# A two-layer graph-attention kernel: the normed input turned by transfers, elu tile by tile from PSUM as h + 1, guards of two heads together, and a plan with other durations

## The chip, the cores and the metric

The kernel runs on one core of one Trainium2 chip. Its time is the device time of one execution in microseconds (us). Five engines work side by side, each in the order of its own queue: TensorE (PE, matmuls), VectorE (DVE), ScalarE (ACT), GpSimd (POOL) and SyncE (SP, which only issues transfers here). A matmul accumulates in one of eight PSUM banks; everything else on the core lies in SBUF.

## The reference, cut to what matters

The input x is (32, 512, 512) in float32, adj is (32, 512, 512) in int32. There are 32 graphs ("batches"), each of 512 nodes with 512 features. Two layers follow each other, and each adds its result to x:

```python
# layer 0
h = relu(layernorm(x))
s = leaky_relu(h @ w_src [:, None] + h @ w_dst [None, :] + b)      # 512 x 512 scores
x = x + softmax(where(adj + eye, s, -inf), axis=-1) @ h
# layer 1: two graph-attention layers, the first with 4 heads of 256 features
h = relu(layernorm(x))
h = elu(gat(h, adj > 0 or eye, W1, heads=4, concat) + b1)          # 512 x 1024
x = x + gat(h, adj > 0 or eye, W2, heads=1) + b2                   # 512 x 512
```

A `gat` projects (h @ W), takes two scores per node and head from the projection, builds leaky_relu(a_src + a_dst) for every pair of nodes, masks it, applies softmax over the sources, and multiplies the weights with the projection. elu(v) is v for v > 0 and exp(v) - 1 below.

## The kernel before, in words

**Tiling.** The 512 nodes of a batch are T = 4 tiles of 128 rows. All matmuls are float32, and each shows in the trace as two instructions.

**Stages of a batch**, by the names of the functions and of the plan's parts:

- `layer0_scores` (S0): layernorm of x (`layernorm`, L555), the normed tiles (`relu_normed`, L573), two dot products per tile, the masks (`masks0`), then `guards` and `edge_weights`.
- `layer0_out` (O0): `attend` multiplies the edge weights with h and adds to x.
- `layer1_in` (I1): layernorm again, the normed tiles `hn`, and their transpose `hT`: four PSUM banks, each filled by four TensorE transposes (`pe_transpose`, L553) and copied out by `evict` (L582: ACT at L586 or DVE at L592, whichever the plan chooses). POOL adds b2 to x (L914), and SP spills x to DRAM.
- `masks1` (M1): loads adj by a transfer on POOL's queue (L802), compares it (L855), clears the diagonal blocks tile by tile (L861), and turns it by a transposing transfer (L812).
- `layer1_project` (P1) and `layer2_project` (P2): the products with W1 and W2 in `products` (L935). It computes a product of 2 x 2 quarters with seven quarter products in place of eight; the sums S1, S2, S3 and S4 of quarters of the left side are made at L968 (DVE) or L969 (POOL), the sums of the weights once at the start (`sums`). Results leave PSUM by `evict` or an addition (L1001).
- `layer1_scores` (S1) and `layer1_head` (H), for each of four heads. In `layer1_head` a tile of 512 x 257 is aggregated at L760 (257th column: the sum of the weights); L1062 takes its reciprocal and L1065 scales, adds b1 and writes `v`. Two tiles share one `v`. elu then works on 512 columns at a time: for heads 0 to 2 (`TURNED`) exp, relu(1 - e) and a maximum (L1079, L1082, L1086), and the result is turned by a transfer; for head 3 exp(v - 1) of v + 1 and a minimum-maximum (L1101, L1105), which gives h + 1, then TensorE transposes, and the eviction takes the 1 off.
- `layer2_out` (O2): `attend` with the second projection, and the store.

**A turn by transfer** (`turned`, L598): ACT packs the 32-bit values into two 16-bit halves (L605), SP issues a transposing transfer (L612), ACT puts the halves together (L621).

**Guards.** `guards` (L682) finds, per node, a bound of the scores, so that the exponent can't overflow: L687 scales the scores, L698 takes a maximum over the masked scores for each tile, L705 and L710 make the guard from it for each head. `in_lines` transposes the guard on TensorE (L652) and stores it as a line, `row_of` loads it back on every partition (L669), and `edge_weights` subtracts it from the mask on POOL (L736), adds the scores on DVE (L741) and takes the exp on ACT (L748).

**The order.** No engine's order is written by hand. Every operation is recorded with its engine (or a choice of two), a duration and the buffers it touches; `Plan.draft` (L160) plays it through once with these durations and always takes, on the engine that is free first, the ready operation of the lowest rank. A rank is the TensorE work recorded before it, less a lead from the table `LEADS` (L52) for its part. The durations are small formulas (`on_pe`, `on_dve`, `on_act`, `by_dma`, ...) or written at the operation: the adjacency load has 8000 ns, or 16000 ns for early ones (L802). Operations marked `lock` on DVE and POOL exclude each other in the draft. Every buffer kind has a fixed number of places (`slots`): 11 of `big` (8 KB per partition: h, hT, projections, edge weights, sums), 4 of `v`, 8 PSUM banks `acc`. Batches overlap: while batch b runs its heads, batch b + 1 runs O0 and I1, batch b + 2 runs S0, and batch b - 1 runs P2 and O2.

## Time and profile before

| what | value |
|---|---|
| time of the runs | 3639.89, 3628.97 and 3638.29 us; median 3638.29 |
| the profiled execution: its own time | 3638.24 us |
| its span, first to last instruction | 3636.5 us |
| granted TensorE clock, mean | 0.994 |
| instructions | 49863 |
| data moved | 412.60 MB, mean 113 GB/s |

The profile lists busy time per engine ("PE" matmuls, "PEld" weight loads that overlap them). A group's line names the source line, engine and operation, the buffers written and read, the count, the busy time in us, the mean in ns, the idle time of the engine ahead of the group, and what ended most of it. A wait's line gives engine, line and what it waited for, then the total in us, the number of times and the longest. A chain's line gives the start and the duration in us of one piece of the work that ended last. A line of the windows gives the stretch, its length, the busy time of PE, PEld, DVE, ACT and POOL (with instruction counts), the granted clock, the share of the DMA engines and GB/s. Means of short instructions include a part that overlaps with the one before.

### The profile page before, as it was taken

The page shows a single profiled execution, that of the slowest core. Times are in us where ns is not written, and L with a number is a line of the kernel's source. Part 1 is how long each engine was busy: PE and PEld are TensorE (multiplying, and loading weights), DVE is VectorE, ACT ScalarE, POOL GpSimd, SP SyncE. Part 2 cuts the span into 40 slices and gives each one's busy share as a digit, 9 for nine tenths or more (in the row PEclk, how much of TensorE's full clock was granted, in tenths as well). Part 3 has the DMA queues.
Part 4 walks back from the last instruction along what each step waited for, and adds up shares of the span by engine and source line. Part 5 has one row for each costly group of instructions (what it writes and reads, how often), then busy time and mean ns, then how long its engine had stood idle before and what let it go on. Part 6 is the DMA issues. An engine that isn't in the chain of part 4 may idle for free.

```text
span 3636.5 us, 49863 instructions
## 1 busy us (share of the span) xinstructions
PE 3487.2 (96%) x16404; PEld 2998.4 (82%) x16404; DVE 2834.7 (78%) x7596; ACT 1891.2 (52%) x3204; POOL 1500.9 (41%) x1394
## 2 busy tenths in 40 slices
PE   3999999999999999999999999999999999999999
PEld 2788888888888888888888888888888888888888
DVE  7997777877777777777777887877787778787775
ACT  2474455555455544555445655545554555554463
POOL 4444334444334443344433444433445334444341
PEclk9999999999999999999999999999999999999999
DMA  6435344443444443444434444344444344444332
GB/s 178 102 95 131 82 125 113 122 124 110 95 114 128 114 112 92 114 128 116 123 87 122 121 122 121 107 98 114 132 121 123 90 120 114 125 119 124 87 111 64
DMA packets 529827, 412.60 MB, mean 113 GB/s; under 512 B 350904, under 2 KB 390048, under 8 KB 529568
## 3 DMA queue, kind: packets, MB, share of 16 engines
q1 hardware_dynamic: 495776, 375.86, 37.3%
q0 software_dynamic: 33792, 33.56, 6.0%
q8 instruction: 129, 2.11, 0.2%
q14 instruction: 130, 1.06, 0.1%
HBM read 290.72 MB, written 68.28 MB: 99 GB/s over the span
## 4 chain that ended last, share of the span: by engine, by line
PE 76%; DVE 10%; DMA 9%; issue 2%; POOL 1%; ACT 0%; SPq 0%; POOLq 0%; DVEq 0%
PE acc L988 37%; PE acc L760 36%; DMA m<-in_adj_dram 8%; DVE junk L698 3%; PE acc L553 2%; DVE big L741 2%; PE acc L652 1%; DMA big<-lines 1%; DVE x L778 1%; DVE col L705 1%; DVE guard L710 1%; DVE st L559 1%; POOL big L736 1%; DVE v L1086 1%; DVE m L855 1%
## 5 line engine op out<-in xcount | busy, mean ns | idle before, releaser
L760 PE MATMUL acc<-big,big 128*128 128x257 f32 (+1 forms) x8192 | 1876.2, 381 | 61.7 <-DVE v L1065 47.8
L760 PEld LDWEIGHTS acc<-big,big 128*128 128x128 f32 x8192 | 1540.8, 190 | 307.1 <-DVE v L1065 59.9
L736 POOL TENSOR_TENSOR big<-m,big 128x512 f32<-128x512 bf16 x768 | 889.6, 1186 | 667.6 <-DMA big<-lines 455.9
L988 PE MATMUL acc<-w_T,big 128*128 128x258 f32 (+1 forms) x3072 | 776.4, 382 | 1.6 <-DVE big L968 1.6
L988 PE MATMUL acc<-w,big 128*128 128x258 f32 (+1 forms) x3072 | 769.2, 381 | 0.9 <-POOL big L969 0.6
L586 ACT COPY big<-acc 128x258 f32<-128x258 f32 (+2 forms) x650 | 248.7, 383 | 871.9 <-PE acc L988 868.8
L748 ACT ACTIVATE big<-big,ac 128x512 f32<-128x512 f32 x768 | 539.9, 719 | 265.6 <-DVE big L741 258.0
L988 PEld LDWEIGHTS acc<-w_T,big 128*128 128x128 f32 x3072 | 582.4, 191 | 91.3 <-DVE big L968 2.0
L988 PEld LDWEIGHTS acc<-w,big 128*128 128x128 f32 x3072 | 572.1, 190 | 87.1 <-ACT big L586 1.0
L741 DVE SCALAR_TENSOR_TENSOR big<-acc,ac,big 128x512 f32<-128x512 f32 x768 | 555.6, 738 | 23.7 <-POOL big L736 20.7
L698 DVE CUSTOM_DVE_ANT_0 junk<-m,acc 128x512 bf16<-128x512 bf16 x768 | 525.1, 684 | 18.5 <-DVE ac L687 0.4
L969 POOL TENSOR_TENSOR big<-big,big 128x512 f32<-128x512 f32 x128 | 187.3, 1464 | 677.1 <-DVE big L968 667.8
L1001 DVE TENSOR_TENSOR big<-acc,big 128x258 f32<-128x258 f32 (+1 forms) x576 | 243.8, 423 | 257.8 <-PE acc L988 219.6
L605 ACT COPY row<-v 128x1024 uint16<-128x1024 uint16 x192 | 199.4, 1041 | 117.1 <-DVE v L1086 113.7
L988 PE MATMUL acc<-w_-T,big 128*128 128x258 f32 (+1 forms) x1024 | 254.3, 380 | 1.9 <-DVE big L1001 1.9
L778 DVE SCALAR_TENSOR_TENSOR x<-acc,r,x 128x256 f32<-128x256 f32 x512 | 237.4, 477 | 21.1 <-PE acc L760 17.7
L1065 DVE SCALAR_TENSOR_TENSOR v<-acc,r,b_r 128x256 f32<-128x256 f32 x512 | 246.0, 481 | 7.4
L586 ACT COPY flat<-acc 8x128 f32<-8x128 f32 (+2 forms) x188 | 48.0, 255 | 357.7 <-PE acc L652 357.7
L621 ACT COPY big<-v 128x1024 uint16<-128x1024 uint16 x192 | 222.3, 1158 | 3.1 <-DMA v<-row 3.0
L988 PEld LDWEIGHTS acc<-w_-T,big 128*128 128x128 f32 x1024 | 191.5, 189 | 33.7 <-DVE big L1001 3.4
L576 ACT ACTIVATE big<-x,col,col 128x512 f32<-128x512 f32 x256 | 195.7, 804 | 23.2 <-DVE col L568 20.4
L1062 DVE RECIPROCAL r<-acc 128x1 f32<-128x1 f32 x512 | 83.9, 164 | 154.7 <-PE acc L760 152.8
(75 smaller groups left out, 2655.2 us busy)
## 6 DMA issues: line engine op xcount, KB each, us to landing
big<-lines SPq DMA_DIRECT2D x380, 256.0 KB
row<-lines SPq DMA_DIRECT2D x190, 256.0 KB
x<-in_x_dram SPq DMA_DIRECT2D x32, 1024.0 KB
m<-in_adj_dram POOLq DMA_DIRECT2D x64, 512.0 KB, 6.9
spill<-x SPq DMA_DIRECT2D x32, 1024.0 KB
x<-spill SPq DMA_DIRECT2D x32, 1024.0 KB
out_dram<-x SPq DMA_DIRECT2D x30, 1024.0 KB
v<-row SPq DMA_TRANSPOSE x192
```

Source lines behind the costliest of these rows:

```text
L586: nc.scalar.copy(dst_of(), src_of())
L605: lambda: nc.scalar.copy(e.at.bitcast(U16).rearrange("p (b f) -> p b f", b=2), values_of().bitcast(U16).rearrange("p (f b) -> p b f", b=2)),
L621: nc.scalar.copy(out.bitcast(U16).rearrange("p k t (n b) -> p k t n b", b=2), values_of().bitcast(U16).rearrange("p (b t k n) -> p k t n b ...
L698: lambda t=t, amax=amax, a_row=a_row: nc.vector.tensor_tensor_reduce(by_blocks(junk), mask_row(mask_max, t), by_blocks(a_row.at), 1.0, LOW ...
L736: lambda t=t: nc.gpsimd.tensor_sub(by_blocks(E.at[:, t, :]), mask_row(mask, t), by_blocks(g_at())),
L741: lambda t=t: nc.vector.scalar_tensor_tensor(E.at[:, t, :], c_row.at, ac.at[:, 4 + j, t : t + 1], E.at[:, t, :], op0=ALU.max, op1=ALU.add),
L748: lambda t=t: nc.scalar.activation(E.at[:, t, :], E.at[:, t, :], AF.Exp, bias=ac.at[:, 2 * j, t : t + 1]),
L760: lambda s=s: nc.tensor.matmul(acc.at[:, :n], E.at[:, s, node_block(t)], of(s), start=(s == 0), stop=(s == T - 1)),
L778: lambda acc=acc, r=r, f=f, t=t: nc.vector.scalar_tensor_tensor(X.at[:, t, f], acc.at[:, :HD], r.at, X.at[:, t, f], op0=ALU.mult, op1=ALU. ...
L988: lambda k=k: nc.tensor.matmul(acc.at[:, :width], at[a]()[:, k, node_block(r)], weight_of(w, k, c), start=(first and k == 0), stop=(k == n ...
L1001: op("DVE", on_dve(width), lambda: nc.vector.tensor_add(place(), acc.at[:, :width], place()), acc(0) + token, token)
L1065: lambda i=i, v=v, acc=acc, r=r: nc.vector.scalar_tensor_tensor(v.at[:, i, :], acc.at[:, :F], r.at, b1_r[:, h * F : (h + 1) * F], op0=ALU. ...
```

## The change

- **Input turned by transfers.** In `layer1_in` each normed tile goes through `turned`; the TensorE transposes and their evictions go.
- **elu a tile at a time, h + 1.** In `layer1_head` every tile of 256 columns is scaled within its PSUM bank (b1 + 1 is added, for all heads), ACT writes exp(. - 1) to `v`, and DVE makes min(v, 1) max the bank: h + 1. The eviction of head 3 no longer subtracts. What the 1 adds to the layer-2 projection is a constant per column, taken off elsewhere: `column_sums` makes the column sums of W2 once by matmul, subtracts them from b2, and its share of the scores, `kappa`, enters layer 2's guards as a shift.
- **Guards of all heads of a call together**: L705's and L710's operations work on both heads at once. The diagonal blocks of a mask are one operation.
- **Places.** The sums of quarters get 6 places of their own (`sum`), `big` has 9, `v` 6, `guard` 8. In `products` two row blocks go through the seven products side by side, on two banks each.
- **The plan.** Leads are given per part (each head its own) and engine; the lock applies to more small operations, and an operation that finds the lock taken is put back; several durations differ (adjacency load 10400 ns and 12600 ns for the first, reciprocal, matmul, score sums). `EARLY` goes. The recording of layer 2's score columns moves ahead of the first `layer1_in`. The branches for `BY_HALVES` and `STATS_BY_ACT` are not used (an empty tuple, and False).

The diff, cut to its core:

```diff
-            rank.append(work - 1e3 * self.LEADS[lead])
+            rank.append(work - 1e3 * self.LEADS.get(lead, 0.0))
...
+            if locks and e in lock and lock["POOL" if e == "DVE" else "DVE"] > at:
+                heapq.heappush(later[e], (lock["POOL" if e == "DVE" else "DVE"], rank[i], i))
+                continue
...
-    one = 2 * max(0.8376 * n + 2, 110.0)
+    one = 2 * max(0.84 * n + 3, 110.0)
...
-        "big": places("big", 11, [P, T * 2 * XL]),
-        "v": places("v", 4, [P, 2, F]),
+        "big": places("big", 9, [P, T * 2 * XL]),
+        "v": places("v", 6, [P, 2, F]),
+        "sum": places("sum", 6, [P, 2, HN]),
...
+    def column_sums():
+        half = KH // 2
+        lo, hi = Buffer("acc"), Buffer("acc")
...
+                    lambda acc=acc, q=q, k=k, at=at, last=len(of) - 1: nc.tensor.matmul(
+                        acc.at[:, :W2], one.to_broadcast([P, P]), w2_s[q][:, k, :],
+                        start=(at == 0), stop=(at == last),
...
+        op(
+            "DVE", on_dve(n * T + 60), lambda: nc.vector.tensor_add(z.at[:, :n, :], ac.at[:, 1 : 2 * n : 2, :], amax.at[:, :n, :]),
+            scores + amax(*every), z(0), lock=True,
+        )
...
-            "POOL", (1100.0, 11000.0) if first else (2200.0, 16000.0 if early else 8000.0), lambda: nc.gpsimd.dma_start(m.at, node_tiles(adj, b)),
+            "POOL", (1100.0, 12600.0) if first else (2200.0, 16000.0 if early else 10400.0), lambda: nc.gpsimd.dma_start(m.at, node_tiles(adj, b)),
...
-        for t in range(T):
-            own = node_block(t)
-            op(
-                "DVE", on_dve(P), lambda t=t, own=own: nc.vector.tensor_mul(m1.at[:, t, own], m1.at[:, t, own], off_diag),
-                m1(t), m1(t), lock=True,
-            )
+        op(
+            "DVE", on_dve(T * P + 70),
+            lambda: nc.vector.tensor_mul(own_blocks(m1), own_blocks(m1), off_diag.rearrange("p (o n) -> p o n", o=1).to_broadcast([P, T, P])),
+            m1(*ROW), m1(*ROW), lock=True,
+        )
...
+        if TURN_INPUT:
             for t in range(T):
-                pe_transpose(
-                    pt, lambda t=t, pt=pt: pt.at[:, node_block(t)], hn(t) + hT("place"),
-                    lambda t=t, k=k: hn.at[:, t, node_block(k)], ident, t,
-                )
-            evict(pt(*ROW), hT(*((k, t) for t in ROW)), lambda pt=pt: pt.at, lambda k=k: hT.at[:, k, :], N)
+                turned(
+                    lambda t=t: hn.at[:, t, :D], both(hn, t), hT("place"),
+                    lambda t=t: hT.at[:, :, node_block(t)].rearrange("p k (t n) -> p k t n", n=P), hT(*((k, t) for k in range(KD))),
+                )
...
-                lambda i=i, v=v, acc=acc, r=r: nc.vector.scalar_tensor_tensor(
-                    v.at[:, i, :], acc.at[:, :F], r.at, b1_r[:, h * F : (h + 1) * F], op0=ALU.mult, op1=ALU.add
+                lambda acc=acc, r=r: nc.vector.scalar_tensor_tensor(
+                    acc.at[:, :F], acc.at[:, :F], r.at, b1_r[:, h * F : (h + 1) * F], op0=ALU.mult, op1=ALU.add
                 ),
-                acc(0) + r(0) + W["b1"](h), v(i),
+                acc(0) + r(0) + W["b1"](h), acc(0),
+            )
+            op(
+                "ACT", on_act(F, 1),
+                lambda i=i, v=v, acc=acc: nc.scalar.activation(v.at[:, i, :], acc.at[:, :F], AF.Exp, bias=minus_one), acc(0), v(i),
+            )
+            op(
+                "DVE", on_dve(F),
+                lambda i=i, v=v, acc=acc: nc.vector.scalar_tensor_tensor(
+                    v.at[:, i, :], v.at[:, i, :], 1.0, acc.at[:, :F], op0=ALU.min, op1=ALU.max
+                ),
+                acc(0) + v(i), v(i),
             )
...
+            pairs = [[Buffer("acc"), Buffer("acc")] for r in range(T // 2)]
+            for which, a, w, begin, then, i, j in (
+                (0, "A11", "11", True, taken, 0, 0),
+                (1, "S1", "T1", True, taken, 1, 1),
+                (0, "S2", "T2", False, taken, 0, 1),
+                (1, "S4", "22", False, added, 0, 1),
+                (0, "S3", "T3", False, added, 1, 1),
+                (1, "A12", "21", True, added, 0, 0),
+                (0, "A22", "-T4", False, taken, 1, 0),
+            ):
+                for r, pair in enumerate(pairs):
+                    product(pair[which], pair[0]("place") + pair[1]("place"), a, w, begin, r, c)
+                    then(pair[which], *dst(i, j, r, c))
```

## The prediction

> **What bounds the kernel now.** I read the page's busy shares first, then the three windows of the span, then the waits of TensorE, then the chain inside one batch.
>
> ```profile
> PE 3487.2 (96%) x16404; PEld 2998.4 (82%) x16404; DVE 2834.7 (78%) x7596; ACT 1891.2 (52%) x3204; POOL 1500.9 (41%) x1394
> ```
>
> ```profile
> 0.00:400.00 400.00, 331.13 (x1515) 278.75 (x1516) 335.45 (x932) 196.19 (x330) 175.68 (x162) 0.97 0.48 122
> 400.00:3400.00 3000.00, 2926.59 (x13812) 2521.74 (x13811) 2343.77 (x6288) 1590.14 (x2700) 1243.62 (x1161) 1.00 0.44 114
> 3400.00:3637.00 237.00, 229.46 (x1081) 197.92 (x1079) 155.47 (x378) 104.83 (x174) 81.61 (x71) 1.00 0.30 86
> ```
>
> TensorE (PE, the first busy column) sets the end. It is busy 3487.2 us of the profiled span of 3636.5 us. Its idle time splits into 400 - 331.1 = 68.9 us in the start, 73.4 us in the 3000 us of steady batches, and 7.5 us in the tail. A batch takes about 111 us, so the steady part loses some 2.7 us per batch. The waits say where:
>
> ```profile
> PE acc L760 <- DVE v L1065: 47.8, 30, 3.9
> PE acc L652 <- DVE guard L710: 36.5, 30, 6.2
> PE acc L553 <- DVE junk L420: 34.0, 4, 29.8
> PE acc L760 <- ACT big L748: 12.7, 3, 6.7
> ```
>
> Each of the first two comes 30 times, once per batch; in the steady window alone they are 45.3 and 28.1 us, together all of its idle time. The other two belong to the start. The chain of one batch shows what makes both:
>
> ```profile
> 1342.12 1.69 DVE col L705
> 1343.82 0.40 DVE x L778
> 1344.21 0.85 DVE guard L710
> 1345.06 0.14 issue
> 1345.19 0.27 PE acc L652
> ...
> 1360.88 11.66 DMA m<-in_adj_dram
> 1372.55 0.02 issue
> 1372.57 0.69 DVE m L855
> ...
> 1374.72 0.41 DVE v L1065
> 1375.13 0.04 issue
> 1375.17 3.50 PE acc L760 x8
> ```
>
> First stall: a four-column addition (L705) takes 1.69 us, while its shortest run in the trace is 0.14; L710 follows late, and PE, in order, stands at the transpose of the guard. Second: the adjacency load takes 11.66 us, VectorE (DVE) stands in order at the mask operation L855, and the head's result behind it (L1065) frees PE's PSUM bank late. The plan had written 174 ns for L705 and 8 us for the load.
>
> **The change, part by part.**
>
> *Input turned by transfers.* Each batch loses 16 TensorE transposes, their four evictions, and gains four turns (ScalarE pack, SP transfer, ScalarE unpack).
>
> ```profile
> L553 PE MATMUL acc<-ident,big 128*128 128x128 f32 x512 | 63.3, 277 | 3.4 <-ACT big L576 3.4
> L592 DVE COPY big<-acc 128x512 f32<-128x512 f32 x91 | 57.5, 685 | 10.1 <-PE acc L553 9.8
> L586 ACT COPY big<-acc 128x512 f32<-128x512 f32 x37 | 20.5, 570 | 2.5 <-PE acc L553 2.5
> L605 ACT COPY row<-v 128x1024 uint16<-128x1024 uint16 x192 | 199.4, 1041 | 117.1 <-DVE v L1086 113.7
> L621 ACT COPY big<-v 128x1024 uint16<-128x1024 uint16 x192 | 222.3, 1158 | 3.1 <-DMA v<-row 3.0
> ```
>
> PE: -63.3 us, all on the bounding engine. DVE: -57.5. ACT: 128 x (1.041 + 1.158) = +281.5, less 20.5. SP: four more transposing issues per batch at a median 1.24 us each.
>
> These are free only while hT is still ready in time. Here a rule is weighed. The Trainium skill, "DMA: Bandwidth & Descriptors", section "Latency and other measured facts", gives a transposing transfer 261 GB/s: 256 KB would take about 1.0 us (an estimate from that page). The trace gives no landing time for it. One unpack early in the run stood idle for its transfer and began 6.2 us after the issue (169.89 to 176.11); others, behind other work of ScalarE (ACT), began 4.1 to 4.9 us after theirs, and one issued at 1357.51, while the adjacency load came in, 9.5 us after. From the last normed tile to hT, transposes and eviction took about 4 x 0.11 + 0.6 = 1.1 us. A turn takes 1.04 + transfer + 1.16: 3.2 us by the rule, 8.4 by the row that waited, 11.7 under the load, so hT comes 2.1, 7.3 or 10.6 us later. In the old order the last transpose ended at 1353.5, its eviction by about 1354.2, and the first projection matmul started at 1364.4, on PE without a wait: 10.2 us of cover. I take the row, 7.3 us, hence nothing on the path. If all batches met the load, 10.6 - 10.2 = 0.4 us per batch, 12 us in all, would show. Behind a turn on SP's queue stand the elu's own turns, the guard rows that GpSimd (POOL) waits for at L736, and x's load and spill.
>
> *elu tile by tile from PSUM.* Per head tile: the scaled STT as before (0.48 us, now written to PSUM), an exp of 256 columns on ACT, and a DVE minimum-maximum of 256. ACT: L1079, L1082 and L1101 go (119.9 + 137.8 + 46.0 = 303.7 us); 512 exps at L1101's 0.719 less 256/1.2 ns, 0.506 us, bring 259. DVE: L1086 and L1105 go (190.1 us); 512 operations at the nearest 256-wide PSUM row, L1001's 0.423 us, bring 216.6, so +26.5. A rule speaks against this: "VectorE: DVE Perf Modes", the section on the TRN2 errata, says that a fixed latency is paid per instruction and advises tiles of at least 512. Halving the tile by its PSUM figure, 120 cycles or 0.125 us, costs at most 256 x 0.125 = 32 us of DVE; the rows say 26.5. Either fits in DVE's idle fifth. What is not hidden by itself is the PSUM bank: it is now held for an exp, a second DVE pass and two hand-overs of about 0.05 us, some 1.0 us more per tile. No row shows a DVE write to PSUM; for ACT the copy into PSUM (L679, 0.58 us) and out of it (L586, 0.57) are alike, so I take nothing; 0.06 us either way, the distance from L1065's 0.481 to L1001's 0.423, would be 31 us of DVE, again inside its idle fifth.
>
> *Guards together, masks in one.* L705 and L710 run 128 times instead of 192: -(81.0 + 56.8)/3 = -46 us of DVE; layer 2's extra shift adds 32 x 0.16 to 0.42, at most 13. Eight diagonal-block operations per batch become two of 512: -58.5 + 64 x 0.7 = -14. Off the path, but the guard is what PE waits for.
>
> *h + 1.* The offset leaves head 3's evictions (0.69 us against 0.57 to 0.69: no difference) and comes back once, as 16 column-sum matmuls, 32 instructions at 0.2175 us, so 7.0 us of PE in the start. They wait for the layer-2 score columns, done near 89 us; the additions of b2 to x (75 us in the old order) move behind them by 15 to 25 us on POOL, and with them the spill of batch 0 and the load of batch 2. The old order reads that at 94.5 us, but its attention is due only a batch period after batch 1's, which began at 87: about 100 us of cover.
>
> *Sums in their own six places, big 11 to 9, v 4 to 6, two row blocks interleaved on four banks.* The same 112 products per batch. The old order has the layer-1 projection at 1364 to 1411 and layer 2's after it, so their sums do not meet. Nothing, for lack of a wait: PE waits 4.4 us at L988 in the whole span.
>
> *The plan.* Guard operations now carry the lock, the load is written as 10.4 us. Of the 27 steady loads in the chain the median is 10.4, and what lies above it adds up to about 11 us. So the second stall falls from 45 to 11 if its place is kept, the first from 28 to about 5, and I allow 0.5 us per batch, 15 us, for a new slip at the new operations: 31 us in place of 73.4. Bounds: 5 us (all but nothing waits) to 90 us (both stalls live on and one more of 0.5 us comes).
>
> **The sum.** PE busy 3487.2 - 63.3 + 7.0 = 3430.9. Idle: start 68.9 + 3 (batch 0's turn has less work beside it: L760 of batch 1 begins at 87, about as late as its hT would; between -10 and +12), steady 31, tail 7.5. Span 3541; the run lies 1.8 us above its span (3638.24 against 3636.5) and at the median of the runs shown (3638.29), so **3542 us**. DVE comes to about 2834.7 - 57.5 + 26.5 - 46 + 10 - 14 = 2754 us (78% of the new span), ACT to 1891 + 281.5 - 20.5 - 303.7 + 259 = 2107 (60%): PE still bounds.
>
> **Rivals.**
>
> *The stalls only move.* TensorE's transposes go, but the waits return elsewhere at the old 73.4 us per steady part: 3430.9 + 71.9 + 73.4 + 7.5 + 1.8 = 3585 us. For it: an in-order plan has slipped twice in every batch, and four more turns can lengthen the load. Against: both slips have a cause that the new numbers name.
>
> *Slower: the PSUM bank.* PE waits already for a bank that L1065 frees late; the new chain runs through two busy in-order queues. Eight banks are shared with four for a projection. If each of the 512 tiles makes PE wait w, the time is 3585 + 512 w: no gain at w = 0.10 us, slower by 0.3% from 0.13, and at 0.15 us 3662. Against: a tile's matmuls take 8 x 0.2175 = 1.74 us, a bank is then held about 3.6 us, and two to three banks carry that.
>
> *The turn is late.* hT misses its cover in every batch by 2 us (several turns under the load in a row): 3585 + 62 = 3647, no change, so what PE no longer transposes it waits.
>
> **Chances and range.** The forecast's case, 3505 to 3575, has 0.66 with its tails; stalls that move 0.20; late turn 0.05; bank 0.09. A difference under 0.3% (11 us) cannot be told from none here. Faster 0.86, same 0.05, slower 0.09. The range takes the low bounds of start and steady part on one side (3542 - 13 - 26, about 3500) and the first rival with a late start and a further slip on the other: 3500 to 3612. Outside lie the two bad cases and thin tails, under 2 in 10.
>
> **What would show it.** PE busy near 3430 with L553 on `big` gone; no 1.7 us run of the guard addition ahead of a waiting transpose; the wait for the mask load at DVE under 20 us (now 58.5); steady PE idle near 31 us. I am wrong if PE's waits name the new min-max or exp of the elu (bank), or the unpack and its transfer (turn), with tens of microseconds.

## The result, and the profile after

The changed kernel takes 3605.05 us, the median of four runs (3597.35 to 3606.86); the kernel before, run beside it, takes 3636.93 us. The ratio is 0.9912, with a 95% interval of [0.989, 0.9933]. So the change gains 0.9%, where 2.6% was forecast: 3542 us was predicted, and 3605 us lies within the range of 3500 to 3612, near its upper end. The line numbers of this section are those of the changed kernel: L464 a dot product, L748 a transpose for a line, L814 the guard, L840 POOL's subtraction of the guard from the mask, L864 the aggregation, L990 the addition of b0 to the scores of layer 0, L1178 the products.

The page's first row and the windows answer to those shown of before:

```profile
PE 3446.4 (96%) x15924; PEld 2946.9 (82%) x15924; DVE 2896.2 (80%) x7650; ACT 1999.0 (55%) x3356; POOL 1464.9 (41%) x1352
```

```profile
0.00:400.00 400.00, 321.59 (x1418) 270.34 (x1419) 323.00 (x926) 201.70 (x331) 152.92 (x147) 0.94 0.48 127
400.00:3400.00 3000.00, 2923.86 (x13563) 2502.39 (x13563) 2441.43 (x6386) 1697.16 (x2858) 1240.66 (x1142) 1.00 0.50 125
3400.00:3605.00 205.00, 201.00 (x945) 174.16 (x943) 131.80 (x339) 100.16 (x168) 71.30 (x64) 1.00 0.36 100
```

TensorE has 16404 - 15924 = 480 instructions less: 512 input transposes gone (one instruction each), 32 instructions of the column sums come (16 matmuls of two). Its busy time fell by 40.8 us where 56.3 was forecast. And in the steady window it still stands idle for 3000 - 2923.9 = 76.1 us; before it was 73.4, and the forecast was 31. The waits of TensorE name the new cause:

```profile
PE acc L748 <- DVE ac L990: 52.8, 28, 2.4
...
PE acc L864 <- ACT big L852: 26.0, 5, 11.7
PE acc L748 <- DVE guard L814: 22.0, 13, 9.4
PE acc L864 <- DVE x L882: 12.5, 20, 1.2
```

The wait for a head's result behind the adjacency load (47.8 us before) is gone, VectorE's own wait for that load too (58.5 us before, none now), and the one for the guard has fallen from 36.5 to 22.0 us. In their place one that did not exist before comes 28 times, about once per batch, and costs 52.8 us: the transpose of layer 0's score line waits for the addition of b0. The timeline of VectorE and POOL shows how it arises (start, duration, engine, line, operation; the accumulator reads between the dots are left out):

```profile
1347.76 0.69 DVE L464 SCALAR_TENSOR_TENSOR junk<-big,ws_r 128x512 bf16<-128x512 f32 x1
...
1348.49 0.69 DVE L464 SCALAR_TENSOR_TENSOR junk<-big,wd_r 128x512 bf16<-128x512 f32 x1
1348.87 7.97 POOL L840 TENSOR_TENSOR big<-m,big 128x512 f32<-128x512 bf16 x6 [4.92 <-DMA big<-lines]
...
1349.30 1.46 DVE L464 SCALAR_TENSOR_TENSOR junk<-big,ws_r 128x512 bf16<-128x512 f32 x1
...
1350.80 1.52 DVE L464 SCALAR_TENSOR_TENSOR junk<-big,wd_r 128x512 bf16<-128x512 f32 x1
...
1352.26 1.11 DVE L990 TENSOR_SCALAR ac<-ac,b_r 128x4 f32<-128x4 f32 x1
...
1353.42 0.27 PE L748 MATMUL acc<-ident,ac 128*8 128x128 f32 x1 [2.05 <-DVE ac L990]
```

Up to 1348.87 a dot takes 0.69 us. From the moment at which POOL starts its subtractions, the next two take 1.46 and 1.52 us and the four-column addition behind them 1.11 us, though it needs 0.22 us alone. That makes some 2.5 us, and PE idles 2.05 us. It is so in every steady batch, and was in none before (first line after, with minimum, median and maximum in ns; second before, with busy time in us and mean in ns):

```profile
L990 DVE TENSOR_SCALAR ac<-ac,b_r x27: 1109/1110/1111, 473.2 to 3326.1; 128x4 f32<-128x4 f32 x27
```

```profile
L882 DVE TENSOR_SCALAR ac<-ac,b_r 128x4 f32<-128x4 f32 x32 | 6.8, 214 | 0.0
```

The plan marks both dots and subtractions with the lock, so in its draft they exclude each other; nothing in the program keeps them apart but the times at which they become ready. POOL became ready when the guard's row had come (1348.87), 3.1 us after SP issued its load at 1345.75; the plan's formula for that load (L764) gives 3.9 us and 262144 bytes at 300 bytes per ns, 4.8 us in all.

In this batch the price has a second part. Windows of 1 us show what TensorE was granted afterwards:

```profile
1352.00:1353.00 1.00, 0.00 (x0) 0.00 (x0) 1.00 (x3) 0.00 (x0) 1.00 (x1) 1.00 0.49 125
1353.00:1354.00 1.00, 0.58 (x4) 0.52 (x5) 1.00 (x6) 0.00 (x0) 0.92 (x2) 1.00 0.82 295
1354.00:1355.00 1.00, 1.00 (x4) 0.82 (x3) 1.00 (x4) 0.86 (x2) 1.00 (x2) 0.52 0.27 104
1355.00:1356.00 1.00, 1.00 (x3) 0.76 (x3) 0.73 (x4) 0.47 (x1) 1.00 (x2) 0.50 0.02 4
1356.00:1357.00 1.00, 1.00 (x4) 0.78 (x3) 1.00 (x4) 0.29 (x1) 0.84 (x1) 0.50 1.09 249
1357.00:1358.00 1.00, 1.00 (x5) 0.85 (x4) 0.72 (x2) 1.00 (x3) 0.00 (x0) 0.78 0.37 124
```

The granted clock (third from the end) falls to half for some 3.5 us after the stall: 3 to 5 matmul instructions per us instead of 6 or 7. The page counts this as busy time. It follows only 5 of the 27 steady stalls (those that end at 1131.7, 1353.4, 1465.4, 1575.5 and 2012.8), and not the longest, of 2.40 us. Each of the five stretches lasts 3.41 us, and their starts (1132.2, 1354.0, 1466.7, 1575.9, 2012.8) lie whole multiples of 3.41 us apart. Cut the steady part on that grid: the piece ahead of each stretch holds 2.00 to 2.08 us of idle time, and no other piece more than 1.93. So a stall of 2 us costs clock here when it falls within one piece, and none when a boundary splits it. Summed over windows of 1 us, busy time times (1 - clock) came to 11.5 us in the steady part before and to 8.4 us after.

From here on, one number serves to compare kernels: the time of a batch, worked out from the steady window, 3000 us x (instructions of TensorE in a batch) / (instructions in the window). A batch has 512 before and 496 after: 3000 x 512 / 13812 = 111.21 us, and 3000 x 496 / 13563 = 109.71 us, of which 2.72 and 2.78 us are idle.

### The profile page after: what moved, and what is told of

Read it like the earlier page. It is cut to its first block, busy times and chain, and to the rows that moved or that the text cites. A ratio compares the mean times of both kernels' runs of the same rounds, so it can differ in the third digit from the quotient of the medians.

```text
span 3604.9 us, 49251 instructions
## 1 busy us (share of the span) xinstructions
PE 3446.4 (96%) x15924; PEld 2946.9 (82%) x15924; DVE 2896.2 (80%) x7650; ACT 1999.0 (55%) x3356; POOL 1464.9 (41%) x1352
## 4 chain that ended last, share of the span: by engine, by line
PE 76%; DVE 10%; DMA 7%; ACT 4%; issue 1%; POOL 1%; SPq 0%; ACTq 0%; DVEq 0%; POOLq 0%
PE acc L864 38%; PE acc L1178 37%; DVE junk L464 3%; DMA row<-lines 3%; DVE junk L796 2%; ACT big L717 2%; ACT big L681 1%; DMA x<-in_x_dram 1%; DMA lines<-flat 1%; DMA out_dram<-x 1%; DVE ac L990 1%; ACT row L701 1%; PE acc L634 1%; PE acc L748 1%; DVE st L662 1%
## 5 line engine op out<-in xcount | busy, mean ns | idle before, releaser
L864 PE MATMUL acc<-big,big 128*128 128x257 f32 (+1 forms) x8192 | 1976.5, 383 | 39.4 <-ACT big L852 26.0
L864 PEld LDWEIGHTS acc<-big,big 128*128 128x128 f32 x8192 | 1539.0, 191 | 296.0 <-ACT big L852 36.6
L840 POOL TENSOR_TENSOR big<-m,big 128x512 f32<-128x512 bf16 x768 | 924.5, 1221 | 711.8 <-DMA big<-lines 381.2
L852 ACT ACTIVATE big<-big,ac 128x512 f32<-128x512 f32 x768 | 542.2, 720 | 291.0 <-DVE big L845 289.1
L845 DVE SCALAR_TENSOR_TENSOR big<-acc,ac,big 128x512 f32<-128x512 f32 x768 | 552.8, 740 | 92.4 <-POOL big L840 63.2
L1178 PE MATMUL acc<-w,big 128*128 128x258 f32 (+1 forms) x2048 | 519.2, 380 | 0.0
L1178 PE MATMUL acc<-w_T,sum 128*128 128x258 f32 (+1 forms) x2048 | 504.9, 381 | 3.0 <-POOL sum L1059 2.0
L1178 PEld LDWEIGHTS acc<-w_T,sum 128*128 128x128 f32 x2048 | 386.6, 190 | 63.2 <-POOL sum L1059 2.8
L1178 PEld LDWEIGHTS acc<-w,big 128*128 128x128 f32 x2048 | 385.5, 189 | 55.4
L1261 ACT ACTIVATE v<-acc,minus_one 128x256 f32<-128x256 f32 x512 | 231.4, 470 | 254.2 <-DVE acc L1254 245.9
L1178 PE MATMUL acc<-w_T,big 128*128 128x258 f32 (+1 forms) x1024 | 263.7, 380 | 0.0
L1178 PE MATMUL acc<-w_-T,big 128*128 128x258 f32 (+1 forms) x1024 | 258.8, 380 | 0.0
L1178 PE MATMUL acc<-w,sum 128*128 128x258 f32 (+1 forms) x1024 | 252.7, 380 | 0.0
L1254 DVE SCALAR_TENSOR_TENSOR acc<-acc,r,b_r 128x256 f32<-128x256 f32 x512 | 242.3, 484 | 4.8
L1265 DVE SCALAR_TENSOR_TENSOR v<-v,acc 128x256 f32<-128x256 f32 x512 | 200.5, 409 | 36.0 <-ACT v L1261 35.7
L1178 PEld LDWEIGHTS acc<-w,sum 128*128 128x128 f32 x1024 | 194.1, 190 | 28.2
```

What stands on the lines that cost most here:

```text
L840: lambda t=t: nc.gpsimd.tensor_sub(by_blocks(E.at[:, t, :]), mask_row(mask, t), by_blocks(g_at())),
L845: lambda t=t: nc.vector.scalar_tensor_tensor(E.at[:, t, :], c_row.at, ac.at[:, 4 + j, t : t + 1], E.at[:, t, :], op0=ALU.max, op1=ALU.add),
L852: lambda t=t: nc.scalar.activation(E.at[:, t, :], E.at[:, t, :], AF.Exp, bias=ac.at[:, 2 * j, t : t + 1]),
L864: lambda s=s: nc.tensor.matmul(acc.at[:, :n], E.at[:, s, node_block(t)], of(s), start=(s == 0), stop=(s == T - 1)),
L1178: lambda k=k: nc.tensor.matmul(acc.at[:, :width], at[a](k // 2)[:, k % 2, node_block(r)], weight_of(w, k, c), start=(begin and k == 0), st ...
L1254: lambda acc=acc, r=r: nc.vector.scalar_tensor_tensor(acc.at[:, :F], acc.at[:, :F], r.at, b1_r[:, h * F : (h + 1) * F], op0=ALU.mult, op1= ...
```

## The experiments

The theory after the first look: TensorE's work has become less by what the transposes cost, but POOL's subtraction of the guard from the mask, started too early, makes VectorE's whole queue late, and TensorE gives the gain back in a new wait. The recorded expectations call this the theory of the port; what stands behind that word comes with elu's last pass below. Rivals: a single transpose stands too early in TensorE's order; the PSUM bank of the new elu; the turn.

**One transpose later.** The order drawn by the plan is kept, and the layer-0 line transposes are moved seven TensorE operations back.

```diff
+        self.put_off(best, ('S0:PE',), 'PE', 7)   # with put_off: shift these operations in best.order, and what hangs on them
```

> The changed kernel with one thing moved: after the plan is drawn, the transpose of layer 0's score line (S0:PE, L748 in the changed kernel) is put behind seven more matmul pairs (3.0 us) on TensorE, with the operations that depend on it; every other order stays. Theory 'uncovered port': the steady stall is that transpose standing for the b0 addition (L990)[...]; with 3 us of cover the wait of 52.8 us goes and nothing takes its place: 3605 - 50 = 3555 us (3545 to 3570). Rival 'stalls move': another chain sets the pace of a batch, PE's idle time turns up at another line: 3590 to 3605 us.

Measured: 3614.41 us, 0.9933 [0.9916, 0.995]; no gain, and slower than even the rival's 3590 to 3605. The wait for the addition is gone, but the steady part has another as large, and the clock loss there is 18.4 us, 10.0 more than in the changed kernel (line numbers of this kernel are 23 higher; L713 copies a line out of a PSUM bank):

```profile
PE acc L887 <- DVE flat L713: 56.8, 27, 2.5
PE acc L887 <- DVE x L905: 11.6, 17, 1.3
```

The dots are as slow as in the changed kernel: 53 of 256 take over 0.9 us, there 54. So it isn't this transpose alone that stands wrongly; VectorE is still late there, and TensorE waits for the next thing that it does.

**The addition of b0 on ScalarE.**

```diff
-            "DVE", on_dve(T), lambda: nc.vector.tensor_scalar(ac.at[:, 1, :], ac.at[:, 1, :], b0_r, None, op0=ALU.add),
+            "DVE", on_dve(T), lambda: nc.scalar.activation(ac.at[:, 1, :], ac.at[:, 1, :], AF.Identity, bias=b0_r),
```

> The changed kernel with the plan untouched and the four-column b0 addition (L990) issued on ScalarE instead of VectorE, at the same place of the order. Theory 'uncovered port': the addition takes about 0.25 us instead of 1.11[...]; the wait at L748 falls from 52.8 to about 27 us (what is left is the two dot products of 1.5 us instead of 0.69 ahead of it): about 3580 us (3570 to 3592). If the addition is late only because what is ahead of it is late, or the stall moves: 3598 to 3608 us.

Measured: 3566.17 us, 0.981 [0.9789, 0.9831]. One short operation out of VectorE's queue brings 39 us, more than the 13 to 35 that were expected: that counted the wait alone, but with 27.9 us of steady idle time the 8.4 us of lost clock go too. The batch takes 108.31 us with 1.74 us of idle time, and no window of the steady part shows a lowered clock. The dots are as slow as in the changed kernel (842 and 873 ns on average, there 843 and 879), so the collision itself is still there, and TensorE waits 24.7 us for a reciprocal (L1251) behind them.

**POOL waits for the addition.** The plan's order is kept; ahead of head 2's first subtraction POOL copies one column that the addition of b0 has written (29 copies in the trace), so that it can't start before it.

```diff
+        def subtract(t):
+            if t == 0 and stage.startswith("S12") and B0_DONE and plan.emitted - B0_DONE[-1][1] < 150:
+                done = B0_DONE.pop()[0]
+                nc.gpsimd.tensor_copy(seen, done.at[:, 1, :1])
+            return nc.gpsimd.tensor_sub(by_blocks(E.at[:, t, :]), mask_row(mask, t), by_blocks(g_at()))
```

> The changed kernel, every order as in the plan, with one tiny GpSimd copy (one column) ahead of head 2's first mask subtraction in a batch (part S12e), which reads the result of the b0 addition: so GpSimd cannot start that subtraction ahead of layer 0's dot products. The plan has it after them (its row load is written as about 4.8 us from issue, the trace shows 3.1), the chip had it 1.7 us earlier[...]. Theory 'port': the last two dot products fall from 1.5 to about 0.7 us, the b0 addition from 1.11 to about 0.2, PE's wait of 52.8 us at L748 goes, and so do the slow-clock stretches behind it: 3605 - 51 - 8 = about 3546 us (3535 to 3560). Rival 'stalls move': the later mask subtraction makes head 2's edge weights late, PE waits at L864 for L852 instead: 3575 to 3605 us.

Measured: 3536.22 us, 0.9722 [0.9706, 0.9738], the fastest kernel of this study and 69 us below the changed one. The place in question, the steady waits and the steady window of this kernel (lines 2 to 12 higher; L1002 is the addition, L844 the copy, L845 the subtraction):

```profile
1435.12 0.69 DVE L466 SCALAR_TENSOR_TENSOR junk<-big,ws_r 128x512 bf16<-128x512 f32 x1
...
1435.86 0.69 DVE L466 SCALAR_TENSOR_TENSOR junk<-big,wd_r 128x512 bf16<-128x512 f32 x1
...
1436.48 0.22 DVE L1002 TENSOR_SCALAR ac<-ac,b_r 128x4 f32<-128x4 f32 x1
1436.77 0.18 POOL L844 COPY seen<-ac 128x1 f32<-128x1 f32 x1 [6.99 <-DVE r L1263]
...
1436.91 3.41 POOL L845 TENSOR_TENSOR big<-m,big 128x512 f32<-128x512 bf16 x3
```

```profile
PE acc L750 <- DVE guard L816: 19.0, 19, 1.8
PE acc L874 <- DVE x L892: 6.6, 11, 0.9
```

```profile
400.00:3400.00 3000.00, 2970.55 (x13861) 2559.31 (x13860) 2438.79 (x6511) 1745.76 (x2930) 1252.88 (x1199) 1.00 0.52 128
```

POOL starts behind the addition and holds up neither dots (0.69 us) nor addition (0.22 us). The wait is gone, idle time in the steady part is 29.4 us, the lost clock 0, and a batch takes 107.35 us. VectorE's busy time falls from 2896.2 to 2841.6 us with the same operations; the 54.6 us were waiting inside instructions. Of the 54 dots that took over 0.9 us in the changed kernel all overlap a subtraction of POOL; here none of 256 takes so long. This is the run that shows the cause: nothing was made cheaper, one engine was made to wait. Of the 2.36 us that the batch gains, 1.73 are idle time and 0.31 lost clock; some 0.3 us of TensorE's busy time stay unexplained.

**The old kernel, two stalls put off.** Does the old kernel owe its stalls to the order as well? Transposes of the layer-2 guards are moved six operations later, the mask comparison seven.

```diff
+        self.put_off(best, ('P2g*',), 'PE', 6)
+        self.put_off(best, ('M1',), 'DVE', 7)
```

> The kernel before, its plan untouched but for two things put later: the transpose of layer 2's guard on TensorE by six matmul pairs (2.6 us), and the compare of the fresh mask (L855) with what depends on it by seven VectorE operations. Nothing of the change is in it. Theory: the two stalls of each batch (73 us in the steady part, and slow matmuls after the longer ones) go: 3637 - 75 = 3562 us (3550 to 3580), so the stalls alone are worth more than the whole change brought. Rival 'stalls move': 3615 to 3637 us.

Measured: 3600.36 us, 0.9897 [0.9881, 0.9914]. Moving a few operations in the old order brings as much as the whole change. About half of the expected gain came (3550 to 3580 us was the theory, 3615 to 3637 the rival), since small waits follow: in the steady part 10.1 us for the same head's result and 7.1 us for a normed tile of the input (L600, `relu_normed`). And yet the batch falls from 111.21 to 109.51 us, 0.99 us of it idle, and no clock is lost:

```profile
400.00:3400.00 3000.00, 2972.75 (x14026) 2551.27 (x14026) 2388.78 (x6378) 1605.51 (x2733) 1257.52 (x1175) 1.00 0.45 116
```

So the old stalls, like the new one, could be taken away by the order alone, without less work.

**Fewer transposes in the old order.** Twelve of a batch's 16 input transposes are left out of the old kernel, and each eviction repeats the one block that is transposed; every queue's order stays.

```diff
-        op("PE", on_pe(P, transpose=True), lambda: nc.tensor.transpose(dst_of(), src_of(), identity), src, dst(part))
+        op("PE", on_pe(P, transpose=True), lambda: issued and nc.tensor.transpose(dst_of(), src_of(), identity), src, dst(part))
...
-                    lambda t=t, k=k: hn.at[:, t, node_block(k)], ident, t,
+                    lambda t=t, k=k: hn.at[:, t, node_block(k)], ident, t, not t,
```

> The kernel before, all orders as they were, with 12 of the 16 input transposes of a batch left out on TensorE (the eviction repeats the one block that is transposed, so the output is not the reference's). It is what the change takes off TensorE, without the turn, without another plan. If TensorE's work sets the pace and the stalls keep their size: 32 x 12 x 0.109 = 42 us less, 3595 us (3588 to 3602). If the two stalls absorb it, since what PE waits for there is set by VectorE and the adjacency load: 3612 to 3637 us, with longer waits at L652 and L760.

Measured: 3679.99 us, 1.011 [1.0084, 1.0136]. Less TensorE work made the kernel slower, which neither expectation had said. Waits over the whole span, and one batch of the chain:

```profile
PE acc L760 <- DVE v L1065: 95.0, 30, 4.7
PE acc L652 <- DVE guard L710: 33.6, 30, 6.2
```

```profile
1373.82 11.35 DMA m<-in_adj_dram
...
1385.19 0.69 DVE m L855
...
1387.34 0.41 DVE v L1065
1387.75 0.04 issue
1387.80 3.42 PE acc L760 x8
1391.21 1.58 PE acc L988 x6
1392.79 1.73 PE acc L760 x8
```

The chain still runs through the adjacency load and VectorE's queue behind it, and TensorE, with less to do, waits the longer for it: 95.0 us instead of 47.8. In the steady part its idle time is 115.7 us, against 73.4. The longer stalls cost the clock more often: eight instructions at half clock take 3.42 us, the next eight 1.73, and the clock loss of the steady part is 39.7 us, against 11.5 in the kernel before. That TensorE is "busy 96%" does not mean that less work ends sooner.

**The turn's transfers left out.** In the changed kernel the 128 transposing transfers of the input are not issued (the unpacking copies what lies there).

```diff
-            lambda: nc.sync.dma_start(
+            lambda: sent and nc.sync.dma_start(
...
+                    False,
```

> The changed kernel, all orders as they were, with the 128 transposing transfers of the input left out (pack and unpack stay; hT then holds untransposed values, so the output is not the reference's). Theory: the turn is hidden in the steady batches, PE waits for none of it; only the start gains: 3592 to 3606 us. Rival 'late turn' or contention: each batch is shorter by 1 us or more: 3575 us or less.

Measured: 3602.91 us, 0.9906 [0.988, 0.9932], the time of the changed kernel. The wait for L990 stands at 51.8 us in the steady part. The turn's transfers and what they do to other loads cost nothing that can be measured in this kernel; that the 76 us of idle time here hide some cost is not ruled out.

**elu's last pass without the bank.** It reads `v` twice instead of `v` and the PSUM bank, so that the bank would be free after the exponential (the maximum with the bank's value is thereby lost).

```diff
-                    v.at[:, i, :], v.at[:, i, :], 1.0, acc.at[:, :F], op0=ALU.min, op1=ALU.max
+                    v.at[:, i, :], v.at[:, i, :], 1.0, v.at[:, i, :], op0=ALU.min, op1=ALU.max
```

> The changed kernel, all orders as they were; elu's last pass (L1265) reads v for both operands in place of v and the PSUM bank, so that the bank is free after the exp, some 0.5 us or more earlier for each of 512 tiles (the output is not the reference's). Theory: the bank is not what PE waits for: 3597 to 3609 us. Rival 'bank': PE gains 0.1 us a tile or more: 3555 us or less.

Measured: 3760.2 us, 1.0337 [1.0319, 1.0355], slower than either expectation. The pass in the changed kernel and in this one:

```profile
L1265 DVE SCALAR_TENSOR_TENSOR v<-v,acc x432: 387/410/424, 475.8 to 3362.2; 128x256 f32<-128x256 f32 x144
```

```profile
L1265 DVE SCALAR_TENSOR_TENSOR v<-v x418: 397/425/2510, 400.5 to 3392.1; 128x256 f32<-128x256 f32 x140
```

With one operand in PSUM it never takes more than 424 ns, though 232 of the 512 passes begin while POOL is at a subtraction or a sum. With both in SBUF the median is nearly the same, but 213 of 512 take over 0.6 us, up to 2.5 us, all while POOL is at a subtraction (131) or a sum of quarters (82): 179 us in all, about what VectorE's busy time grows by (172 us). So the run says nothing on the bank, and much on the other question: what POOL holds up is a VectorE operation that reads SBUF alone. The Trainium skill states a rule for this ("SBUF — State Buffer", "SBUF: two separate sides"): a VectorE operation with two SBUF inputs, against a GpSimd operation that reads SBUF, shares one pair of ports, and the one that starts second waits for the whole of the other; a VectorE operation in a mode that uses two ports does so too. This case's numbers fit: L464 and the subtraction both read SBUF alone, one subtraction takes 1.16 us in the median, and a dot that meets it takes 0.8 us more. The addition of b0 has one tensor as input and is held as well; which of the page's two cases it is, no run here shows. And not all that reads SBUF is held: 58 of the layer norm's statistics (L662, one input) began beside a subtraction or a sum, and none took over 697 ns, where 676 is the median alone.

**The bank once more, in the mended kernel.** The pass is left out altogether (v is the exponential alone). This run and the next two are from another chip than the mended kernel's own; the kernel before takes 3633.05 us there, 3638.94 beside the mended kernel.

```diff
-                lambda i=i, v=v, acc=acc: nc.vector.scalar_tensor_tensor(
+                lambda i=i, v=v, acc=acc: None and nc.vector.scalar_tensor_tensor(
```

> The kernel of the run with the waiting mask subtraction (3536 us), and in it the last VectorE pass of the elu, the minimum-maximum of 256 columns that reads the PSUM bank, is left out 512 times; v is then the exponential alone, so the output is not the reference's. VectorE loses some 512 x 0.41 = 210 us and each bank of a head comes free after the exponential, about 0.5 us earlier. My theory: TensorE's own work sets the end, and only the waits of some 29 us in the steady part are left to win: 3510 to 3530 us, with the same 2970 us of TensorE work in a steady window now a little higher. Rival (the PSUM bank, or VectorE's load as such, costs more than the waits show): 3490 us or below.

Measured: 3537.28 us, 0.9747 [0.9714, 0.9781], no gain, though VectorE's busy time falls to 2702.0 us. Steady idle time goes from 29.4 to 23.2 us. It is a little outside the upper end of what the theory gave (3510 to 3530), since most of the remaining waits stayed, and far from the rival's 3490: the bank and VectorE's load as such are no bound here.

**What a transpose is worth.** Sixteen unused transposes of a constant per batch are added to the mended kernel.

```diff
+                    extra and s == 0 and nc.tensor.transpose(acc.at[:, :P], ident, ident),
```

> The same kernel of 3536 us, with one extra 128 x 128 transpose of a constant, unused, ahead of the first matmul of each head tile of layer 1: 16 in a batch, 512 in all, as many as the change took off TensorE. If TensorE's work sets the end once the plan's slip is mended, the time goes up by 512 x 0.109 = 56 us, to about 3592 us. If idle time of TensorE absorbs some of it, by less: 3545 to 3570. If it disturbs the order and the clock drops as in the old kernel with fewer transposes, by more than 65 us.

Measured: 3602.64 us, 0.992 [0.9892, 0.9948]: 66 us more than the mended kernel by the medians and 72 by the ratios, where 56 was expected; the interval of this ratio alone is 10 us to either side. It reaches the third case's 65, but that case's sign, a lowered clock, is absent (nothing lost in the steady part).

```profile
400.00:3400.00 3000.00, 2966.81 (x14055) 2538.39 (x14054) 2403.57 (x6405) 1713.01 (x2872) 1224.21 (x1174) 1.00 0.52 125
```

The batch goes from 107.35 to 3000 x 512 / 14055 = 109.28 us. Of these 1.93 us, 0.16 are more idle time; 1.77 us, 0.111 us for each, are the transposes. Over the 27.5 batches of the window that is 53 us, and over all 32 it would be 62; the rest lies in the start, the tail and the spread of the runs. Once the slip is mended, then, TensorE's work does set the end, and each transpose costs what it takes.

**The largest wait left.** In the mended kernel the transposes of the layer-1 guards are moved six operations later.

```diff
+        self.put_off(best, ('S10g:PE', 'S12g:PE'), 'PE', 6)
```

> The same kernel of 3536 us, with the transposes of the layer 1 guards six TensorE operations later in TensorE's order, since their wait for the guard (19 us of the 29 us that TensorE is idle in the steady part) is the largest left. If that wait stands alone, 3518 to 3525 us. If it is the late VectorE queue as a whole, as it was when one transpose was put off alone, the next wait takes its place and the time stays at 3530 to 3545 us.

Measured: 3539.13 us, 0.9747 [0.9719, 0.9776]. The guard's wait is gone from the steady part, whose idle time is 21.4 us instead of 29.4, and the time is the same, as the second expectation had it: 8 us less of waiting do not come out at the end.

**Two plans drawn anew.** The changed kernel with its transposes back, and the changed kernel with a shorter duration for the row load: 2.2 + 0.87 = 3.1 us by the formula in place of 4.8.

```diff
-    TURN_INPUT = True
+    TURN_INPUT = False
```

> The changed kernel with the input transposed on TensorE again (TURN_INPUT False), the plan drawn anew with the same leads. Theory: the turn takes 16 transposes of 0.109 us off TensorE per batch, 56 us, and costs about 11 us in the start: without it 3605 + 45 = 3650 us, give or take 25 us for another plan. Rival 'late turn': the turn costs as much by lateness as it saves, 3590 to 3610 us without it.

```diff
-            "SP", by_dma(4 * P * N, 3900.0),
+            "SP", by_dma(4 * P * N, 2200.0),
```

> The changed kernel with the plan's duration of a row load (256 KB broadcast from one line of DRAM) written as 2.2 + 1.7 = about 3.9 us less than before, near the 3.1 us from issue to use that the trace shows, instead of 4.8 us; the plan is drawn anew with it, nothing else differs. If the wrong duration is what makes the mask subtractions start early beside the scores' addition, and the plan then keeps them apart by its lock, the wait for that addition goes and the time falls to 3545 to 3575 us. If a plan drawn anew only places its slips elsewhere, 3590 us or more, as in the run without the turn.

Measured: 4262.41 us, 1.1724 [1.1697, 1.175], and 4077.52 us, 1.1228 [1.1193, 1.1263]. Both are inconclusive on what they were to test. In the second, TensorE waits 170.5 us in the steady part for the guard (61 times) and 70.0 us for the same addition L990, at a granted clock of 0.95. In both, one thing changed and the plan drawn anew with the same leads gave an order that is worse by far. So that the row load's duration is what let POOL start early stays argued from the timeline: its 3.1 us against 4.8 us are shown, that mending the number mends the plan is not.

## Why the prediction was wrong, point by point

**The step that failed** is in *The plan*: "I allow 0.5 us per batch, 15 us, for a new slip at the new operations: 31 us in place of 73.4". What it said of the two old stalls came: the one behind the load went, the guard's fell to 10.1 us in the steady part. The new slip was mis-sized: 50.9 us in the 27 steady batches, 1.9 us each, not 0.5, and the runs show what it is, the dots and the addition of b0 held up by POOL's subtraction. So the likeliest case didn't come but its first rival, *the stalls only move*, with idle time of 76.1 us where it took 73.4. The upper bound that the step itself named, 90 us, held it. The rival was given 0.20. The old profile offered no place for the new slip (there the addition of b0 takes 0.21 us), but it held the same collision at another operation, the four-column addition L705 whose 1.69 us the prediction read as a first stall without asking what makes it:

```profile
L705 DVE TENSOR_TENSOR col<-ac,col 128x4 f32<-128x4 f32 x192 | 81.0, 422 | 0.0
```

```profile
1340.40 4.63 POOL L736 TENSOR_TENSOR big<-m,big 128x512 f32<-128x512 bf16 x4
1342.04 1.78 DVE L705 TENSOR_TENSOR col<-ac,col 128x4 f32<-128x4 f32 x1
```

The first line gives a mean of 422 ns over all 192 runs. Of the 61 over 0.4 us, 58 overlap a subtraction of POOL (L736); of the 131 shorter ones, 2 begin beside one. In the changed kernel, whose guard operations carry the lock, the same addition (L803) has 4 long runs in 128. But the lock acts in the draft, by durations that are not the chip's, and a new order is a new draw of what meets: the dots carry the lock too, and were caught, and the addition of b0 behind them carries none.

**Where the other 20 us to that rival's 3585 come from**, by the profiled execution (the prediction's own terms add up to 3543, not 3542, which changes nothing): TensorE's busy time is 3446.4, not 3430.9 (+15.5); the start idles 78.4, not 71.9 us (+6.5); the steady part 76.1, not 73.4 (+2.7); the tail 3.9, not 7.5 (-3.6). Together +21.1.

- *Transposes.* The 63.3 us were the group's busy time. By the run with sixteen extra ones a transpose costs 0.111 us, 512 of them 56.6 us: 6.7 us too much.
- *Column sums.* 7.0 us were forecast at full clock; they took 6.2 + 3.8 = 10.0 us. Half of them ran from 34 to 41 us, at the start of TensorE's work, and of those 16 instructions the first eleven took 629 to 796 ns each, where the later half took about 380.
- *Clock in the start.* By windows of 1 us it cost 11.3 us of busy time, before 5.3 (its record begins at 39.9 us here, at 53.9 before). With transposes and column sums, and 3.1 us less lost in the steady part, that makes some 12.6 of the 15.5 us; the rest is open.
- *Start.* +3 us was taken, with bounds of -10 and +12; the idle time grew by 9.5 us. The first 110 us hold as much of it in both kernels (TensorE is busy 49.3 us in each, at a granted clock of 0.84 here and 0.92 before). The growth comes between 110 and 400 us, and 7.3 us of it are one wait, until 203.8, for an exponential of edge weights (L852). Without the turn's transfers the same wait is 7.3 us too; why ScalarE and VectorE come to it late was not tried.

**What held.** The turn's transfers cost nothing on the path of the changed kernel (without them: same time). elu tile by tile lies in VectorE's idle share: 512 passes of 0.409 us where 0.423 was taken, the first pass into PSUM at 0.484 us as out of it (0.481), and the exponential 0.470 where 0.506 was; leaving one pass out altogether brought nothing, so the forecast's rival of the PSUM bank has nothing for it. What halving the tile costs VectorE did not reach the path, whether one takes the row's 26.5 us or the 32 us that the prediction estimated from the skill's figure; the two passes took 200.5 and 190.1 us, but some 15 of the old pass's were waiting beside POOL, so the row comes nearer. VectorE's total was forecast at 2754 and came to 2896 us; 54.6 us of the excess vanish when POOL waits. A part of the other 87 is the same collision elsewhere: a four-column operation of the layer norm (L673) takes 41.1 us in all, where it took 10.5 before (L568), and its 29 long runs all overlap POOL. ScalarE came to 1999 us, 108 under the forecast, off the path.

**The state that was forecast exists.** With POOL made to wait, the batch's idle time is 29.4 us in the steady part (forecast 31) and the time 3536 us (forecast 3542). That TensorE's work and its idle time make up the time was right, and what the prediction undervalued is what a plan's order does when one operation comes earlier than written. That the idle time agrees to 2 us is in part luck: the forecast made it of 11 us behind the load, 5 at the guard and 15 of a new slip, and the run made it of nothing behind the load, 19.0 at the guard and some 10 at other places.

## What to carry to other kernels

When the order of the queues comes from a model of durations, price a change by the batch it would make with its slips mended, and give a new slip of the old size a fair chance when the draft's durations are not the chip's; here two stalls per batch before were followed by one after. Ask of every instruction that is long in some runs and short in others what ran beside it: that question, put to L705, would have named the collision before the change. Look for pairs that the model keeps apart only by time (here VectorE and POOL reading SBUF at once) and make the cheap one wait by a real dependency: one 0.18 us copy on POOL was worth 69 us. And measure a freed bound with both signs, work taken away and work added; in an order full of slips, taking TensorE work away made the kernel slower.

## What the runs showed of the hardware that had not been expected

- A VectorE operation on SBUF operands that meets POOL's subtraction grows from 0.69 to 1.46 and 1.52 us, a four-column one from 0.22 to 1.11 us, and passes of 256 columns from 0.42 to up to 2.51 us; with one operand in PSUM the same pass stays below 0.43 us. The profile shows no wait for this, only a longer instruction.
- TensorE's clock falls to half for 3.41 us at a time, on a fixed grid of 3.41 us. Worked out from the clock's record in the steady part of eight kernels that show such drops (before, changed, and six of the runs), no piece at full clock was followed by another at full clock when it held over 2.04 us of idle time, and none by half clock when it held under 1.73 us. A stall of 2.40 us across a boundary cost none. The Trainium skill ("TensorE: Matmul & The Clock Gate", "What's actually happening") puts the drop after an idle window of some 3.4 us, the window running free of the kernel; the grid agrees, but here a window idle for some 2 us of its 3.41 was enough, and one window at half clock was all that each of the five stalls cost. A stall that is caught costs some 1.7 us more (8.4 us in five), and the profile counts that as busy.
